# Third attention of a four-layer kernel: inverted softmax sums spread through DRAM by DMA and multiplied by GpSimd, in place of a product on TensorE

## The chip, the cores and the metric

The kernel runs as one launch on one core of a Trainium2 chip. The metric is the device time of the launch in microseconds. Before the change it is 2238.06 us, the median of three runs (2237.61 to 2240.51).

## The reference

Four layers, each an attention and a feed-forward network, are applied to 1024 rows of 256 numbers; every one of the eight parts is `x = layernorm(x + part(x))`. The change is in the third attention alone:

```python
def _L2_attn_ref(x, W_qkv, W_proj):
    ...
    SCALE = 1.0 / np.sqrt(D).astype(np.float32)
    b, s, d = x.shape
    qkv = x @ W_qkv.T
    q, k, v = jnp.split(qkv, 3, axis=-1)
    q = q.reshape(b, s, H, HD).transpose(0, 2, 1, 3)
    ...
    attn = jnp.einsum('bhqd,bhkd->bhqk', q, k) * SCALE
    causal = jnp.tril(jnp.ones((s, s), dtype=bool))
    attn = jnp.where(causal[None, None], attn, -jnp.inf)
    probs = jax.nn.softmax(attn, axis=-1)
    out = jnp.einsum('bhqk,bhkd->bhqd', probs, v)
    out = out.transpose(0, 2, 1, 3).reshape(b, s, d)
    return out @ W_proj.T
...
x = _layernorm(x + _L2_attn_ref(x, L2_attn_W_qkv, L2_attn_W_proj), axis=-1)
```

The input is one sequence of 1024 rows, so the attention is causal over all of them. There are 16 heads of 16 numbers. The softmax over the keys needs, for every head and query, the sum of the exponentials; the output of the head is divided by that sum. How the inverse of that sum reaches the 16 rows of its head is what the change alters.

## The kernel before, in words

`four_layers` runs eight stages one after the other; `attn2` is the fifth (from about 960 to 1190 us of the profile). Everything is float32, in part split into two rounded halves.

**Layout in `attn2`.** The heads are taken four at a time (`ch`, 0 to 3) and the queries in two halves of 512 (`half`). A pair (ch, half) is a unit; the units run in the order (0,0), (1,0), (2,0), (3,0), (0,1), (1,1), (2,1), (3,1). In a unit, `attend` goes over the blocks of 128 keys that the causal mask allows (4 in half 0, 8 in half 1). For a block it makes the transposed scores of two pairs of heads on TensorE into tiles of the PSUM pool `wide` (three buffers; L1629, and L1635, which adds minus the maxima), ScalarE exponentiates them into `pt` (L1641), GpSimd zeroes the masked half of a block on the diagonal (`affine_select`, L1644), and TensorE multiplies the values of the heads by `pt` into the unit's accumulator `out` (`apply`, L1616). A head has 32 rows of the accumulator: 16 of output, and row 16 of each 32 is the sum of the exponentials, because the values carry a column of ones there.

**Maxima beside it.** For a later unit, `maxima` makes the scores in the other orientation (L1582, with the mask added on TensorE by L1589) in the same three `wide` buffers, and VectorE takes their row maxima (L1593, joined by L1598). At the end of a unit's maxima, VectorE copies them (L1602), TensorE transposes them (L1605), and ScalarE and VectorE make the tile `tall` (L1608, L1609) that the unit's L1635 reads.

**What `finish` does.** When a unit's accumulator is complete, ScalarE copies it to the SBUF tile `sums` (pool `ot`, L1658). Four DMAs on SyncE's queue take the four rows of sums into `inv`, 128 partitions of 16 (L1661). After four steps VectorE inverts `inv` in one small instruction (L1667), and four DMAs put the inverses back into the rows of `sums` (L1669). Four steps later TensorE multiplies `pick` (which copies row 16 of each 32 to all 32) by `sums` into a `wide` tile (L1676; a float32 product is two passes), and VectorE multiplies `sums` by it (L1677). For ch = 3 the output projection (L1701), the residual, the layernorm and the transposes of the half follow, a step each. The last unit (3,1) has a shorter ending of its own, `finish_last`, which the change leaves alone. There are so seven calls of `finish`; below they are F1 to F7 in the order of the units.

**What sets the order.** The stage runs inside `k.in_order()`: the instructions of TensorE, VectorE, ScalarE and GpSimd stand in the order in which Python issues them. Each `yield` of the generators is one step: after every pair of heads in `attend`, the loop in `attn2` advances the maxima (`ahead`), the placing of queries and keys (`placing`), the second half's projections and values (`beside`) and the ending of the unit before (`ending`). The first `next(ending)` comes at the unit's end and the others one a step of the next unit. SyncE's DMAs are not in that written order; a scheduler places them in the one queue of SyncE, where a DMA that waits holds back those behind it. A DMA on that queue also uses one of eight semaphores in turn, so it can have to wait for the eighth DMA before it.

**Other work on the queues at the time of F1 and F2.** `second_half` stores split projections to DRAM with sixteen DMAs of 256 KB (L1531, SyncE), and GpSimd loads them back in another arrangement (`load_rows`, L1542, eight DMAs). SyncE also reloads weights of the next stage as buffers come free (L103). The tiles of `second_half` come from the pool `parts`, six buffers in a ring.

Of the kernel before, what the change touches and what calls it, by code (L numbers as in the profile page):

```python
# [28 lines left out]
ALU = mybir.AluOpType  # L29
AX = mybir.AxisListType  # L30

P = 128
# [4 lines left out]
HALF = 512  # L37
# [1367 lines left out]
def attn2(k, a):  # L1405
# [15 lines left out]
    nc = k.nc  # L1421
# [30 lines left out]
    pick = k.tile("const", [P, P], tag="pick")  # L1452
# [14 lines left out]
    projected, parts, placed, whole = {}, {}, {}, set()  # L1467
# [98 lines left out]
    def rows(j, n=32):  # L1566
        return slice(n * j, n * j + n)
# [86 lines left out]

    def finish(ch, half, out, outs):

        sums = k.tile("ot", [P, HALF])
        nc.scalar.copy(sums, out)  # L1658
        inv = k.tile("st", [P, 16], tag="inv", bufs=2)
        for j in range(4):  # L1660
            nc.sync.dma_start(  # L1661
                out=inv[rows(j), :],
                in_=sums[32 * j + 16 : 32 * j + 17, :].rearrange("p (c e) -> p c e", e=16),
            )
        for _ in range(4):
            yield
        nc.vector.reciprocal(inv, inv)  # L1667
        for j in range(4):
            nc.sync.dma_start(  # L1669
                out=sums[32 * j + 16 : 32 * j + 17, :].rearrange("p (c e) -> p c e", e=16),  # L1670
                in_=inv[rows(j), :],
            )
        for _ in range(4):
            yield
        ps = k.wide()[:, :HALF]
        nc.tensor.matmul(ps, lhsT=pick, rhs=sums, start=True, stop=True)  # L1676
        nc.vector.tensor_tensor(sums, sums, ps, ALU.mult)  # L1677
        outs.append(sums)
        yield
        if ch < 3:  # L1680
            return
        stats = k.tile("st", [P, 4, 2])
        for s in range(4):
            project_out(half, s, outs)
            yield
            k.add_stats(4 * half + s, stats)
        rstd = k.power(stats[:, :, 1], 4, LN_EPS)
        for _ in range(2):
            yield
        for s in range(4):  # L1690
            k.norm_tile(4 * half + s, stats, rstd[:, s : s + 1])
            if s % 2:
                yield
        for t in (0, 2):
            k.transpose_two(t, split=True)
            yield

    def project_out(half, s, outs):
        y = k.bank()[:, :D]
        for i in range(4):  # L1700
            nc.tensor.matmul(  # L1701
                y, lhsT=outs[i][:, s * P : (s + 1) * P], rhs=wo[:, i, :],
                start=i == 0, stop=i == 3,
            )
        k.add_rows(4 * half + s, y)
# [19 lines left out]
    with k.in_order():  # L1725
# [45 lines left out]
        for ch, half in units:  # L1771
            while (ch, half) not in found:
                next(ahead)
            out = k.bank()
            for step, _ in enumerate(attend(ch, half, out)):
                next(ahead, None)
                if half == 0 and step % 4 == 3:
                    next(ahead, None)
                if step % 2:
                    next(placing, None)  # L1780
                if (ch, half, step) > (0, 0, 1) or half:
                    next(beside, None)
                next(ending, None)
            for _ in ending:
                pass
            if (ch, half) != units[-1]:
                ending = finish(ch, half, out, outs[half])
                next(ending)
# [524 lines left out]
```

## Time and profile before

| what | value |
|---|---|
| median of three runs | 2238.06 us |
| the profiled execution, as timed | 2230.16 us |
| its span, first to last instruction | 2228.5 us |
| mean granted TensorE clock | 0.972 |
| L1676, TensorE products with `pick` | 14 passes, 7.6 us busy |
| L1677, VectorE multiplies | 7, mean 683 ns |
| L1667, VectorE reciprocals of `inv` | 7, median 242 ns |
| L1661 and L1669, gathers and scatters on SyncE's queue | 28 each, issue median 590 and 538 ns |

The profiled execution is 7.9 us below the median of the runs, and its span 1.66 us below its own time. Times in the text are microseconds from the start of the span. A row of groups reads: line, engine, operation, tile written and tiles read, shapes, count; then the busy time, the mean of one in ns, and the time for which the engine stood idle just before these instructions, with what ended it. A line of the view of waits reads: who waited, for whom, total us, times, longest. The view of windows gives the busy time of each engine in a stretch with the number of instructions, then the granted TensorE clock, the mean busy share of the DMA engines and GB/s.

Where the seven endings lie (start and end in us):

| | copy L1658 | gathers L1661 issued | inverse L1667 | scatters L1669 issued | product L1676 | multiply L1677 |
|---|---|---|---|---|---|---|
| F1 | 1020.58 | 1021.20 to 1023.71 | 1030.03 | 1030.56 to 1033.03 | 1037.09 to 1038.19 | 1038.77 |
| F2 | 1041.23 | 1041.84 to 1044.83 | 1048.25 | 1048.57 to 1051.01 | 1055.84 to 1056.96 | 1057.76 |
| F3 | 1058.54 | 1059.16 to 1061.60 | 1068.49 | 1068.76 to 1071.19 | 1074.34 to 1075.42 | 1076.14 |
| F4 | 1076.84 | 1077.45 to 1079.89 | 1082.76 | 1083.03 to 1085.47 | 1088.18 to 1089.31 | 1089.40 |
| F5 | 1110.57 | 1111.18 to 1113.62 | 1118.15 | 1118.43 to 1120.87 | 1123.87 to 1124.95 | 1125.61 |
| F6 | 1139.23 | 1139.85 to 1142.29 | 1144.97 | 1145.24 to 1147.68 | 1151.50 to 1152.52 | 1153.09 |
| F7 | 1161.44 | 1162.06 to 1164.50 | 1165.65 | 1165.97 to 1168.41 | 1169.68 to 1170.78 | 1170.82 |

### The profile page before, as it was taken

To read this page: it belongs to the slowest core of one execution; us is meant where nothing else is said; L and a number is where in the kernel's file an instruction comes from. 1 tells how busy PE (TensorE), PEld (TensorE's weight loads), DVE (VectorE), ACT (ScalarE), POOL (GpSimd) and SP (SyncE) were. 2 spreads that over 40 slices of the span, in tenths; PEclk is the share of its full clock that TensorE was granted. 3 is DMA by queue.
4 is the path that set the end of the run, shared out by engine and by line. 5 is a ranking of instruction groups with operands and counts; after the bars stand their busy time and mean duration, and the time that the engine had idled before them with its cause. 6 is when DMAs were issued, how large, how long until landed. Compare 5 with 4: busy or idle time off the path is not lost.

```text
span 2228.5 us, 24592 instructions
## 1 busy us (share of the span) xinstructions
PE 2037.2 (91%) x7893; PEld 1191.4 (53%) x7893; DVE 1299.4 (58%) x2588; ACT 849.6 (38%) x2230; POOL 522.3 (23%) x771
## 2 busy tenths in 40 slices
PE   7988768899999997988988998899999989999997
PEld 3655544576766665754434443466666665433343
DVE  6898756677777664456754444277777664222223
ACT  3656424453444433444462223654444441111111
POOL 5343131333333332402110000433333320000000
PEclk9999879999999999999999999999999999999998
DMA  6222443253545542105000000034355321222211
GB/s 183 76 72 58 136 130 109 64 148 102 145 108 161 144 103 78 38 29 181 1 2 10 29 30 0 24 95 111 93 141 125 91 53 63 76 76 84 76 65 44
DMA packets 152520, 186.88 MB, mean 84 GB/s; under 512 B 31460, under 2 KB 115240, under 8 KB 152392
## 3 DMA queue, kind: packets, MB, share of 16 engines
q1 hardware_dynamic: 142808, 160.25, 26.2%
q0 software_dynamic: 9584, 25.05, 3.7%
q8 instruction: 64, 1.05, 0.2%
q14 instruction: 64, 0.52, 0.1%
HBM read 85.24 MB, written 17.44 MB: 46 GB/s over the span
## 4 chain that ended last, share of the span: by engine, by line
PE 62%; DVE 9%; DMA 7%; ACT 3%; issue 3%; POOL 2%; SPq 1%; DVEq 0%; POOLq 0%; ACTq 0%
PE bank L159 19%; PE wide L274 9%; PE bank L408 8%; PE wide L307 6%; DMA by<-factors 5%; PE bank L166 4%; PE bank L1179 2%; DVE turned L371 2%; PE bank L1616 2%; PE bank L856 2%; PE bank L1019 1%; DMA pt<-turned 1%; PE bank L1354 1%; POOL p L267 1%; PE wide L1629 1%
## 5 line engine op out<-in xcount | busy, mean ns | idle before, releaser
L159 PE MATMUL bank<-xT,w 128*128 128x512 f32 (+2 forms) x1488 | 629.2, 563 | 4.1 <-DVE xT L185 3.0
L159 PEld LDWEIGHTS bank<-xT,w 128*128 128x128 f32 (+1 forms) x1488 | 283.1, 194 | 275.1 <-issue 254.3
L371 DVE STREAM_TRANSPOSE turned<-p 128x128 f32<-128x128 f32 (+7 forms) x232 | 283.5, 1222 | 76.0 <-DMA pt<-turned 40.3
L274 PE MATMUL wide<-k,q 128*128 128x512 f32 (+3 forms) x768 | 293.7, 492 | 18.3 <-ACT p L259 17.5
L267 POOL TENSOR_SCALAR p<-p,st 128x128 f32<-128x128 f32 (+7 forms) x256 | 190.5, 744 | 475.3 <-DVE st L266 474.8
L408 PE MATMUL bank<-pt,v 128*128 128x256 f32 x1216 | 279.4, 371 | 8.0 <-DMA pt<-turned 5.7
L408 PEld LDWEIGHTS bank<-pt,v 128*128 128x128 f32 x1216 | 225.9, 191 | 60.6 <-issue 21.0
L254 DVE TENSOR_REDUCE st<-wide 128x1 f32<-128x128 f32 (+7 forms) x256 | 193.4, 756 | 47.1 <-PE wide L279 40.1
L307 PE MATMUL wide<-t,w 128*128 128x512 f32 (+1 forms) x392 | 196.7, 626 | 17.0 <-DVE t L2205 11.8
L274 PEld LDWEIGHTS wide<-k,q 128*128 128x128 f32 x768 | 139.5, 191 | 135.3 <-issue 92.9
L259 ACT ACTIVATE p<-wide,st,factor 128x128 f32<-128x128 f32 (+7 forms) x128 | 106.4, 831 | 213.5 <-POOL st L256 210.6
L2204 DVE TENSOR_TENSOR t<-t,bank 128x512 f32<-128x512 f32 (+1 forms) x66 | 45.3, 686 | 238.8 <-PE bank L159 238.8
L259 ACT ACTIVATE p<-wide,st 128x128 f32<-128x128 f32 (+7 forms) x128 | 94.9, 741 | 230.1 <-DVE st L254 211.9
L2203 ACT ACTIVATE t<-bank 128x512 f32<-128x512 f32 (+1 forms) x66 | 39.4, 597 | 305.5 <-PE bank L159 279.5
L307 PEld LDWEIGHTS wide<-t,w 128*128 128x128 f32 (+1 forms) x392 | 67.8, 191 | 134.3 <-DVE t L2205 58.4
L779 ACT ACTIVATE e<-wide,st 128x128 f32<-128x128 f32 x256 | 90.0, 377 | 74.3 <-DVE st L787 65.6
L166 PE MATMUL bank<-w,xT 128*128 128x512 f32 (+2 forms) x288 | 118.0, 547 | 0.0
L249 DVE TENSOR_TENSOR wide<-wide,causal 128x128 f32<-128x128 f32 x192 | 55.9, 291 | 98.7 <-PE wide L274 97.5
L1641 ACT ACTIVATE pt<-wide 128x1024 f32<-128x1024 f32 (+3 forms) x96 | 75.6, 811 | 69.9 <-PE wide L1635 68.1
L166 PEld LDWEIGHTS bank<-w,xT 128*128 128x128 f32 x288 | 52.6, 196 | 44.0 <-issue 40.3
L1593 DVE TENSOR_REDUCE st<-wide 128x2 f32<-128x1024 f32 x64 | 64.3, 1020 | 20.0 <-PE wide L1589 10.2
L845 PE MATMUL bank<-w,ot 128*128 128x256 f32 x256 | 67.4, 411 | 6.8 <-ACT ot L839 5.5
(307 smaller groups left out, 2788.4 us busy)
## 6 DMA issues: line engine op xcount, KB each, us to landing
by<-factors SPq DMA_DIRECT2D x64, 256.0 KB
pt<-turned SPq DMA_DIRECT2D x60, 240.0 KB
pt<-turned SPq DMA_DIRECT2D x60, 176.0 KB
pt<-turned SPq DMA_DIRECT2D x156, 64.0 KB
w<-in_L_ffn_gate_up_dram SPq DMA_DIRECT2D x16, 512.0 KB
pt<-turned SPq DMA_DIRECT2D x28, 256.0 KB
pt<-turned SPq DMA_DIRECT2D x60, 112.0 KB
pt<-turned SPq DMA_DIRECT2D x28, 224.0 KB
```

Of the source, the lines that this page charges most:

```text
L159: self.nc.tensor.matmul(out, lhsT=weight(c), rhs=self.xcols(c, lo, n), start=c == 0, stop=c == NC - 1)
L166: self.nc.tensor.matmul(out, lhsT=self.xcols(c, lo, n), rhs=weight(c), start=c == 0, stop=c == NC - 1)
L254: nc.vector.tensor_reduce(top, scores[:, :n], axis=AX.X, op=ALU.max, negate=True)
L259: nc.scalar.activation(probs[:, :n], scores[:, :n], AF.Exp, bias=top, scale=1.0 if scale is None else scale, accum_out=total,)
L267: self.nc.gpsimd.tensor_scalar(probs[:, :n], probs[:, :n], total, 1.0, ALU.mult, ALU.mult)
L274: self.nc.tensor.matmul(s[:, lo : lo + m], lhsT=query, rhs=key(lo, m), start=True, stop=not masked or lo + m < n, skip_group_check=masked,)
L307: nc.tensor.matmul(acc[m][:, half * HALF : (half + 1) * HALF], lhsT=down[:, m * P : (m + 1) * P], rhs=h, start=i == 0, stop=i == count - 1,)
L371: k.nc.vector.transpose(squares.rearrange("p b (k q) -> p b k q", q=32), probs[:, :n].rearrange("p (k i b) -> p b k i", b=4, i=32),)
L408: self.k.nc.tensor.matmul(out.rearrange("p (a q) -> p a q", q=32) if first else out.rearrange("p (s a q) -> p s a q", s=2, q=32), lhsT=val ...
L779: nc.scalar.activation(e[:, r, f, b, :], sc[:, r, f, b, :], AF.Exp, bias=top[:, at : at + 1], accum_out=total[:, at : at + 1],)
L845: nc.tensor.matmul(y, lhsT=oT[:, i % 2 * 2 + i // 2].rearrange("p b n -> p (b n)"), rhs=wo[:, i, :], start=i == 0, stop=i == 3,)
L1641: nc.scalar.activation(two[:, :, lo:], sc[:, :, lo:], AF.Exp)
```

## The change

The four gathers stay. The inverse now comes two steps after them in place of four. One DMA stores the 128 x 16 inverses to a DRAM row for each of the four heads; two steps later one DMA reads the four rows back, each repeated to 32 partitions, into a new SBUF tile `spread` of 128 x 512 from the ring `parts`; three steps later GpSimd multiplies `sums` by it. The four scatters, the product with `pick` (and its `wide` tile) and VectorE's multiply go. From the first `next` to the multiply there are seven yields in place of eight, so that all that follows in `finish` comes a step earlier.

```diff
-        for _ in range(4):
+        for _ in range(2):
             yield
         nc.vector.reciprocal(inv, inv)
-        for j in range(4):
-            nc.sync.dma_start(
-                out=sums[32 * j + 16 : 32 * j + 17, :].rearrange("p (c e) -> p c e", e=16),
-                in_=inv[rows(j), :],
-            )
-        for _ in range(4):
+        row = k.tile("dram", [4, HALF], tag=f"inv_{ch}{half}")
+        nc.sync.dma_start(out=row.rearrange("j (p e) -> (j p) e", e=16), in_=inv)
+        for _ in range(2):
             yield
-        ps = k.wide()[:, :HALF]
-        nc.tensor.matmul(ps, lhsT=pick, rhs=sums, start=True, stop=True)
-        nc.vector.tensor_tensor(sums, sums, ps, ALU.mult)
+        spread = k.tile("parts", [P, HALF])
+        nc.sync.dma_start(out=spread, in_=row.unsqueeze(1).to_broadcast([4, 32, HALF]))
+        for _ in range(3):
+            yield
+        nc.gpsimd.tensor_tensor(sums, sums, spread, ALU.mult)
         outs.append(sums)
```

An empty line is added at the head of `finish`, so that lines below it have other numbers after the change: the copy is L1659, the gathers L1662, the inverse L1668, the store L1670, the spread L1674, the multiply L1677.

## The prediction

> **What bounds the kernel now.** I read first the busy shares, then the stage that the change touches, window by window, then the groups of its lines, the waits, and last the timeline around each of the seven endings, F1 to F7. The page:
>
> ```profile
> PE 2037.2 (91%) x7893; PEld 1191.4 (53%) x7893; DVE 1299.4 (58%) x2588; ACT 849.6 (38%) x2230; POOL 522.3 (23%) x771
> ```
>
> ```profile
> core 0: us, PE busy (x) PEld busy (x) DVE busy (x) ACT busy (x) POOL busy (x), PEclk, DMA share, GB/s
> 1020.00:1040.00 20.00, 17.71 (x123) 8.07 (x122) 13.58 (x22) 7.56 (x12) 6.25 (x12) 1.00 0.85 263
> 1040.00:1050.00 10.00, 8.83 (x72) 5.29 (x70) 6.42 (x11) 5.00 (x7) 4.51 (x8) 1.00 0.74 227
> ...
> 1110.00:1140.00 30.00, 26.08 (x205) 12.19 (x204) 22.99 (x37) 15.11 (x20) 3.24 (x8) 1.00 0.01 2
> ...
> 1160.00:1170.00 10.00, 8.43 (x65) 3.81 (x62) 0.25 (x1) 8.59 (x11) 0.77 (x2) 1.00 0.02 2
> ```
>
> TensorE is busy for 83 to 98% of each of the stage's stretches, VectorE for up to 77%; GpSimd has room. The DMA engines are nearly full from 1020 to 1050 us, where F1 and F2 lie (0.85 and 0.74), and empty after 1070. So a microsecond off TensorE is worth about one, and a wait of VectorE costs only what the three `wide` buffers don't cover. What goes:
>
> ```profile
> L1676 PE MATMUL wide<-ot,pick 128*128 128x512 f32 x14 | 7.6, 626 | 1.7 <-DMA ot<-inv 1.6
> L1677 DVE TENSOR_TENSOR ot<-ot,wide 128x512 f32<-128x512 f32 x7 | 4.8, 683 | 5.1 <-PE wide L1676 4.9
> ```
>
> The waits for the gathers, before:
>
> ```profile
> DVE inv L1667 <- DMA inv<-ot: 11.9, 1, 11.9
> ```
>
> The reciprocal waits once, in F7, where VectorE has no more maxima. In the other six the gather had landed when VectorE came to it. How narrowly is seen in F2:
>
> ```profile
> 1044.00 1.23 DVE L1593 TENSOR_REDUCE st<-wide 128x2 f32<-128x1024 f32 x1 [0.46 <-PE wide L1582]
> 1045.43 0.42 DVE L1593 TENSOR_REDUCE st<-wide 128x2 f32<-128x256 f32 x1 [0.20 <-PE wide L1589]
> 1045.89 0.16 DVE L1598 TENSOR_TENSOR tops<-st 128x2 f32<-128x2 f32 x1
> 1046.22 1.82 DVE L1593 TENSOR_REDUCE st<-wide 128x2 f32<-128x1024 f32 x2 [0.17 <-PE wide L1582]
> 1048.08 0.16 DVE L1598 TENSOR_TENSOR tops<-st 128x2 f32<-128x2 f32 x1
> 1048.25 0.25 DVE L1667 RECIPROCAL inv<-inv 128x16 f32<-128x16 f32 x1
> ```
>
> F2's last gather packet ended at 1047.64. In F7, where VectorE did wait, the packets ended at 1165.31 and the reciprocal began at 1165.65: 0.34 us from packet to start. F2's gather was thus usable at 1047.98, 0.27 us before its reciprocal.
>
> **What the skill says.** "DMA: Bandwidth & Descriptors", section "Why a DMA increments its semaphore by 16 and not by 1": a transfer is split over the largest number of engines up to 16 that divides the slowest dimension of both sides. The spread has 4 rows on its DRAM side, so 4 engines. The trace agrees in the last stage, where L2201 spreads two rows to 128 partitions, 128 packets of 2 KB at 84 ns each: on two engines that is 64 x 84 ns = 5.4 us, and its issue takes
>
> ```profile
> L2201 SPq DMA_DIRECT2D by<-factors x66: 498/4724/7113, 1838.1 to 2184.5; - x66
> ```
>
> with a median of 4.7 us[...]. On 16 engines it would be 0.7. "GPSIMD Engine Reference", section "3.1 Elementwise — side-by-side cycle accounting", has a two-input product there about twice as long as on VectorE; this trace has one of the same shape:
>
> ```profile
> L1854 POOL TENSOR_TENSOR decoded<-sign,scales x24: 1261/1272/1285, 434.8 to 866.5; 128x512 f32<-128x512 f32 x24
> ```
>
> "SBUF — State Buffer", section "SBUF: two separate sides", says that GpSimd and a two-input VectorE operation exclude each other; VectorE's two-input operations here (L1598) are 0.16 us long, so I cost it at 0 (up to 0.2 in all).
>
> **Part 1, TensorE's product goes.** Two passes take 1.0 to 1.1 us. F4, F5, F6: the next work follows at once; 1.06 + 1.00 + 0.95 = 3.0. F1: after it the chain of maxima waits for VectorE (L1605 waited 0.99 for L1602), so what is saved is L1677's 0.68 ahead of L1602; 0.65. F2, F3: VectorE runs without a gap just after, so between 0.65 and 1.06; 0.8 each. F7: TensorE also waited 1.25 for the scatter and ScalarE then 2.53 for TensorE, so both go: 2.3. Sum 3.0 + 0.65 + 1.6 + 2.3 = 7.6 (if each gave its all, 7.7 + 1.7 = 9.4). VectorE's 4.8 us are worth only the part counted here.
>
> **Part 2, the reciprocal moves two steps up.** Now the gather is what VectorE waits for; behind it in VectorE's order stand the maxima, and behind them TensorE's next `wide` tile. The order of the built instructions gives the new place; from the timeline, when VectorE would be there, and when the gather is usable (last packet + 0.34):
>
> F1 1024.33 against 1024.86; F2 1045.23 against 1047.98; F3 1062.41 against 1062.75; F4 1080.38 against 1081.04; F5 1115.64 against 1114.78; F6 1142.78 against 1143.44; F7 unchanged.
>
> Waits of 0.5, 2.75, 0.3, 0.7, 0, 0.7. What reaches TensorE: F1 0.4, since L1602 stands right behind and L1605 waits for it. F3, F4, F6: the next maximum used to wait 0.2 to 0.5 for TensorE anyway and the reciprocal's own 0.24 leaves its old place; with three buffers TensorE notices 0.2, 0.2 and 0.3. F2 is the large one: the tile after next must go into the buffer that the delayed maximum (old start 1045.43) still holds, so TensorE, at 1046.0, stops until 1048.7: 2.7. It can be more: the gather's fourth DMA now waits by its semaphore for the 512 KB reload (before, for a 256 KB store), and F1's spread sits ahead of it on four engines; 0 to 2 more, I take 0.6, so 3.3. Less is possible if the queues drain sooner (2.0). Sum 0.4 + 3.3 + 0.2 + 0.2 + 0.3 = 4.4; bounds 2.6 and 7.
>
> **Part 3, store, spread and GpSimd.** Quiet queues: the store lands 1.65 us after issue (the same kind, L1984: issue 1836.36, SyncE free of its wait at 1837.98); the spread's first packet comes 1.37 after issue (L2201: 1838.09 to 1839.46), 32 packets on each of four engines take 2.7, and 0.35 to the semaphore: 4.4. Inverse to spread is 6.1 us, with the product 7.4. On SyncE the spread waits for the store, holding back whatever follows: in F1 two stores of `second_half` (whose data come later anyway), in F2 a reload; 0. GpSimd's queue behind the multiply has the `affine_select`s, and TensorE's L1616 waits for them. F2, F3: GpSimd comes to the multiply at 1055.1 (+2.7) and 1073.8, the spreads land near 1056.6 (full queues, 4 us more) and 1069; 0. F4: product done at 1088.7; the projection, now at the place of L1676 (1088.2), needs this head group as its fourth, 1.3 us later; 0, and 0.5 if late. F5 to F7 have over 4 us or no selects near. F1 is tight: spread issued near 1029 behind about 1 MB, 4 us of queue, 2.7 of packets, half again for GpSimd's loads beside it: near 1037. The multiply then ends at 1038.4, the select at 1038.8, and L1616 wants it by 1040.1. Cover 1.2 us; 0. The 28 small scatters that go lighten the queues; 0.
>
> **Sum.** -7.6 + 4.4 + 0 = -3.2 us against the profiled execution's 2230.16 us (span 2228.5), so 2227.0 there; the median of the runs is 7.9 above that execution, and the difference carries over: 2238.06 - 3.2 = 2234.9.
>
> **Rivals.** A: the early reciprocal costs nearly nothing, as the gathers land earlier with 28 DMAs gone and VectorE 4.8 us lighter. For it: four of the waits are under 0.7 us. Against: F2's gather was late behind GpSimd's loads, which stay. Then -7.6 + 1 = -6.6: 2231.5. B, slower: F1's spread drowns in the full queues. Place: GpSimd, its multiply ahead of the last select of unit (1,0). It costs from a landing at 1038.3 on, one for one at L1616; and F2's first gather waits by its semaphore for this same spread, so beyond 1041.5 F2's reciprocal moves too. Landing at 1045 costs 6.7 and puts F2's gather about 3 later: -3.2 + 9.7 = +6.5, 2244.6. For it: DMA share 0.85 and L2201's slow kind. Against: F1's scatters, issued at 1030.56, were done at 1036.49. That the change doesn't do what it says is excluded by the order of the instructions.
>
> **How the numbers follow.** My forecast 0.52 (own range 2231.5 to 2238.5), A 0.23, B 0.25 (from 2238.5 to 2246). The range takes A from 2230 and B to 2242.5. A measurement of this kernel tells about 0.2%, 4.5 us, from no change, so faster is below 2233.6: A's 0.22 and 0.10 of the forecast, 0.32; slower is above 2242.5: half of B, 0.14; the rest 0.54.
>
> **What would show it.** The reciprocal's row idle for the gather in F1, F2, F4, F6, longest in F2 (3 us), with TensorE idle there; no gap of TensorE in F7 near 1168; spreads of 4.4 us in F3 to F7; no L1616 waiting for GpSimd in F1. Wrong would make me: F2's wait under 1 us, or above 6; L1616 idle on L1644; TensorE's wait at L1701 in F4.

## The result and the profile after

The changed kernel takes 2241.89 us (median of 20 runs, 2237.17 to 2250.01) against 2237.91 for the kernel before in the same set (20 runs, 2233.33 to 2242.46): ratio 1.002, 95% interval 1.001 to 1.0029. It is about 4 us slower, clear of the noise, where 3.2 us less was predicted. The profiled execution of the changed kernel took 2238.66 us (span 2236.7) against 2230.16, so these two stand 8.5 us apart; part of that is chance, as will be seen. In what follows, differences in us are of medians; the ratios and their 95% intervals are taken from all the runs and can stand up to 2 us away from them.

From F1's copy to the copy of the last unit the stage took 159.13 us before and 163.97 after. The page after, engine totals:

```profile
PE 2036.8 (91%) x7879; PEld 1192.9 (53%) x7879; DVE 1294.2 (58%) x2581; ACT 850.2 (38%) x2230; POOL 530.7 (24%) x778
```

TensorE has 14 instructions fewer, but 0.4 us less to do and not 7.6. The view of windows, the changed kernel, stretches that answer to those of before (moved by 4.8 us at F1 and about 9 at the end):

```profile
core 0: us, PE busy (x) PEld busy (x) DVE busy (x) ACT busy (x) POOL busy (x), PEclk, DMA share, GB/s
1025.34:1045.34 20.00, 16.60 (x112) 7.91 (x112) 12.94 (x20) 7.56 (x12) 7.46 (x13) 0.96 0.81 251
1045.34:1055.34 10.00, 9.31 (x47) 5.71 (x46) 5.95 (x10) 4.95 (x6) 3.58 (x7) 0.50 0.74 235
1119.00:1149.00 30.00, 26.66 (x213) 12.44 (x211) 22.15 (x35) 17.20 (x22) 4.52 (x9) 1.00 0.04 11
1169.00:1179.00 10.00, 9.74 (x76) 4.35 (x80) 0.25 (x1) 8.74 (x10) 0.25 (x1) 1.00 0.07 17
```

The second row is what the prediction did not have. TensorE is busy 93% of it and does only 47 products in 10 us, where the row of before for 1040 to 1050 has 72: its granted clock (the column after POOL) is 0.50, half of full speed, for the whole stretch. "Half clock" below means this. The groups of the changed kernel between 985 and 1195 us (last column: idle time ahead, and for whom):

```profile
L1677 POOL TENSOR_TENSOR ot<-ot,parts 128x512 f32<-128x512 f32 x7 | 8.9, 1272 | 54.4 <-DMA parts<-inv 51.6 <-DMA rows<-parts 2.8
...
L1598 DVE TENSOR_TENSOR tops<-st 128x2 f32<-128x2 f32 x32 | 6.5, 203 | 1.1
L1605 PE MATMUL wide<-ident,tops 128*128 128x128 f32 x32 | 5.8, 310 | 8.7 <-DVE tops L1602 8.7
...
L1602 DVE COPY tops<-tops 128x8 f32<-128x8 f32 x16 | 2.8, 205 | 0.0
L1668 DVE RECIPROCAL inv<-inv 128x16 f32<-128x16 f32 x7 | 1.8, 251 | 17.3 <-DMA inv<-ot 17.3
```

The same groups before:

```profile
L1598 DVE TENSOR_TENSOR tops<-st 128x2 f32<-128x2 f32 x32 | 5.5, 173 | 1.1
...
L1605 PE MATMUL wide<-ident,tops 128*128 128x128 f32 x32 | 5.0, 280 | 5.4 <-DVE tops L1602 4.2 <-ACT pt L1641 1.2
...
L1602 DVE COPY tops<-tops 128x8 f32<-128x8 f32 x16 | 2.5, 185 | 0.0
```

GpSimd's multiply and the late inverse are there as expected. New are three things: TensorE waits 8.7 us, not 4.2, for VectorE's copies L1602 ahead of its transposes L1605; the small operations L1598 and L1602 have become slower on average; and in F7 L1616 waits 2.00 us for GpSimd.

**A pause and what follows it.** The changed kernel's TensorE ahead of L1605 of unit (3,0), then two windows, the first over that pause (3.41 us), the second after it:

```profile
1041.24 0.28 PE L1589 MATMUL wide<-causal_b,ident_b 128*128 128x128 bf16 x2
1041.45 0.64 PE L1616 MATMUL bank<-pt,v 128*32 128x256 f32 x8
1044.55 1.09 PE L1605 MATMUL wide<-ident,tops 128*128 128x128 f32 x4 [2.46 <-DVE tops L1602]
```

```profile
1040.39:1043.80 3.41, 1.52 (x16) 0.51 (x14) 3.41 (x5) 0.17 (x1) 0.76 (x1) 1.00 0.99 299
1043.80:1057.46 13.66, 12.21 (x54) 7.86 (x54) 7.04 (x13) 4.95 (x6) 5.39 (x10) 0.50 0.76 234
```

The same place before, with full clock after it:

```profile
1039.75 0.63 PE L1605 MATMUL wide<-ident,tops 128*128 128x128 f32 x4 [0.99 <-DVE tops L1602]
```

In this stage of the traces the half-clock stretches are 3.4 us long or multiples of that, 6.8, 10.2, 13.7 and once 17.1, and in each trace they all begin on one grid of 3.41 us, which lies differently against the program from trace to trace. The Trainium skill, "TensorE: Matmul & The Clock Gate", section 'Part 1: The HAM clock gate (the "warmup" mystery)', describes this: TensorE's clock is halved after an idle window of about 3.4 us, and the windows run free of the program. The traces agree on the length and on the free running. They differ in that a window needn't be idle (TensorE was busy for 1.52 of 3.41 us above), and there the measurement decides. I divided all 17 traces of this study into those windows (30 to 2200 us of each) and counted in each the columns of its products, a product weighted by the share of the 128x128 array that it uses (32 columns of weights count a quarter, 64 rows a half; a well-filled window has some 4,000):

```
weighted columns in a window at full clock   windows   followed by half clock
under 900                                        119   119
900 to 1200                                      148   135
1200 to 1500                                     237    33
1500 to 2100                                     324    16
over 2100                                       9282    23
```

All 23 windows of the last row lie between 952 and 1090 us, so in this stage the weighting does not tell the windows apart well. The time for which TensorE was busy in the window does so at least as well: half clock followed all 198 full-clock windows with under 1.25 us of it, 107 of the 290 with 1.25 to 2 us and 21 of the 9622 with more; in the stage alone (985 to 1200 us) 10 of 10, 24 of 31 and 7 of 945. The traces so show that too little work in a window brings half clock. They don't show that a narrow product counts less than a full one.

So a pause of 2.5 us, with 1.5 us of work around it, is enough if a window happens to lie over it. As the windows run free, the same kernel meets it in some executions and not in others: in F7 of the changed kernel half clock followed a pause of 2.0 us in one trace, and none followed a pause of 1.8 us in the other. A good part of the scatter of the times goes with this: among the 65 runs of the kernel before in the third set below, each thousandth of the whole launch's mean clock goes with 1.1 us (the slope; the correlation is -0.76).

### The profile page after: what moved, and what is told of

It reads as the page before. It is cut to its first block, busy times and chain, and to the rows that moved or that the text cites. A ratio compares the mean times of both kernels' runs of the same rounds, so it can differ in the third digit from the quotient of the medians.

```text
span 2236.7 us, 24533 instructions
## 1 busy us (share of the span) xinstructions
PE 2036.8 (91%) x7879; PEld 1192.9 (53%) x7879; DVE 1294.2 (58%) x2581; ACT 850.2 (38%) x2230; POOL 530.7 (24%) x778
## 4 chain that ended last, share of the span: by engine, by line
PE 60%; DVE 10%; DMA 8%; ACT 3%; issue 3%; POOL 2%; SPq 1%; DVEq 0%; POOLq 0%; ACTq 0%
PE bank L159 18%; PE wide L274 9%; PE bank L408 8%; PE wide L307 6%; DMA by<-factors 5%; PE bank L166 4%; PE bank L1179 2%; DVE turned L371 2%; PE bank L856 2%; DMA pt<-turned 2%; PE bank L1616 1%; PE bank L1019 1%; PE bank L1354 1%; POOL p L267 1%; PE wide L1582 1%
```

## The experiments

Three theories. Clock: the time that TensorE saves is spent waiting at L1605 for VectorE, which has not become faster, and the longer pauses halve its clock. Wait: the new waits alone cost it. Queue: the spread is late or GpSimd's multiply is in the way. Each kernel was compared with the kernel before on the same chip in the same set; the kernel before itself had medians from 2237.45 to 2244.59 in these sets, so each difference is taken within a set, and two kernels of different sets are compared by these differences. "Stage" is from F1's copy to the last copy in the profiled execution; "lost" is the time in it times the share of clock not granted (3.4 us of half clock is 1.7 lost). An "idle product" is one whose result nobody reads.

**First set: undo or do one part.** The control:

> The kernel before, unchanged, against itself: the size of the scatter, and the granted clock of each of its runs, which the page of one execution doesn't give. All theories: 0 us within about 2. The clock theory (half-clock stretches of TensorE are what the changed kernel loses by) expects a mean clock near 0.970 here, clearly above the 0.9635 of the changed kernel's runs; the wait theory (the early reciprocal and GpSimd's late product make TensorE wait) has no need of it and expects about the same 0.964.

Measured: 2245.16 against 2242.96, ratio 1.0003 (0.9994 to 1.0013). Mean clock 0.966 and 0.967, lower than the 0.970 that the clock theory expected but above the changed kernel's 0.9636. Stage 160.61 us, 5.1 lost; before's first profile 159.13, 3.4 lost. Six of its seven units agree with that profile to 0.02 us; the third, F3 to F4, is 1.46 longer, with 1.7 more lost. So a unit's length is a fine measure as long as the clock is named beside it.

The changed kernel with the inverse at four steps:

```diff
-        for _ in range(2):
+        for _ in range(4):
             yield
         nc.vector.reciprocal(inv, inv)
```

> The changed kernel with the reciprocal and all that follows it back at four steps after the copy (nine yields to the product in place of seven). Wait theory: the early reciprocal holds up VectorE, so some 4 us come back: 3 to 5 us below the changed kernel, near or a little below the kernel before. Clock theory: the reciprocal's place matters little, 0 to 1.5 us, and the kernel stays 3 to 4 us above the one before with a mean clock near 0.9635. Queue theory (the spread's late landing holds GpSimd's selects): the spread lands two steps later but the product is also two steps later, so 0.

Measured: +8.0 us (1.0034, 1.0021 to 1.0046; five runs), mean clock 0.960. All theories missed. The inverse no longer waits (but in F7), and yet nothing comes back. The clock is 0.0072 lower than that of the kernel before; at 1.1 us per thousandth that is an estimate of 7.9 us, the whole difference. Three pauses at L1605 are 1.82, 1.82 and 2.35 us, stage 159.75 with 8.5 lost.

The kernel before with only the inverse (and scatters) two steps up:

```diff
-        for _ in range(4):
+        for _ in range(2):
             yield
         nc.vector.reciprocal(inv, inv)
...
-        for _ in range(4):
+        for _ in range(6):
             yield
         ps = k.wide()[:, :HALF]
```

> The kernel before with only the reciprocal and the scatters moved two steps up; the product with pick and VectorE's multiply stay in their places. Wait theory: 4 us slower than the kernel before (F2 most, TensorE idle there about 3 us). Clock theory: 0 to 1 us. Queue theory: 0.

Measured: +8.5 us (1.0036, 1.0024 to 1.0049), mean clock 0.9637 against 0.967. That is more than any of the three theories had. The waits of VectorE for the gather are the predicted ones, F2's (timeline of VectorE):

```profile
1064.97 0.25 DVE L1667 RECIPROCAL inv<-inv 128x16 f32<-128x16 f32 x1 [1.98 <-DMA inv<-ot]
```

But the stage, 162.38, is only 1.8 above the control's 160.61 at the same 5.1 lost, nearly all in F2 (19.19 us to F3's copy against 17.31). The lower clock is worth an estimated 3.6 us. The other 3 us are not shown by this execution; the pauses at L1605 grew to 1.50 and 2.33 us.

The kernel before without the product:

```diff
-        ps = k.wide()[:, :HALF]
-        nc.tensor.matmul(ps, lhsT=pick, rhs=sums, start=True, stop=True)
-        nc.vector.tensor_tensor(sums, sums, ps, ALU.mult)
         outs.append(sums)
```

> The kernel before without the product with pick and without VectorE's multiply in the seven endings: it leaves out the division by the sums for those seven units; gathers, reciprocal and scatters stay. It is the upper bound of what the change can take off TensorE. By the prediction's part 1: 7.6 us below the kernel before (6.5 to 9.4). Clock theory: less, 2 to 5 us, with a lower mean clock than the kernel before[...].

Measured: -3.2 us (0.9994, 0.9986 to 1.0003), mean clock 0.9637. By the ratio it is less still, and the interval reaches no gain at all: less than half of the 7.6, with the lower clock, as the clock theory has it. Why the clock was lower this set doesn't show; the windows above point to the longer pause at (3,0), 1.82 us for 0.99. From F4 on, where its trace has no half clock, the four units are shorter by 0.94, 0.90, 0.84 and 2.35 us; the prediction had 1.06, 1.00, 0.95 and 2.3.

**Second set: the pause filled, and the pause made longer.** Products that nobody reads, in the wait:

```diff
         ps = k.wide()[:, :HALF]
+        if (ch, half) in ((3, 0), (0, 1), (3, 1)):
+            for _ in range(4):
+                nc.tensor.matmul(
+                    ps, lhsT=keys[0][:, 0, :P], rhs=queries[0][:, 0, :HALF],
+                    start=True, stop=True, skip_group_check=True,
+                )
         for s in range(4):
             nc.tensor.transpose(ps[:, s * P : (s + 1) * P], top[:, s, :], k.ident)
```

> The changed kernel with four idle products (keys by queries, 128x128 by 512 columns, into the wide tile that the transposes then overwrite) put on TensorE ahead of the transposes L1605 of the units (3,0), (0,1) and (3,1), where its trace has TensorE waiting 2.46, 2.52 and 2.09 us for VectorE; they lie in the wait. Clock theory (such a pause leaves a window of about 3.4 us nearly without work, after which TensorE is granted half its clock for 3.4 to 13.7 us): the half-clock stretches behind these three places go, the mean clock comes up to 0.967 or more, 5 to 8 us faster than the changed kernel, so 1 to 4 us below the kernel before. Wait theory (the pauses themselves are the whole cost): 0 to 1 us slower than the changed kernel, clock as it was.

Measured: level with the kernel before (2238.66 against 2238.58; 1.0004, 0.9992 to 1.0015), mean clock 0.9676 against 0.9679. TensorE does more work than in the changed kernel, and that kernel's 4 us above the kernel before are gone. The 1 to 4 us below it that the clock theory had were not reached. Its TensorE at the same place as above, and the windows over the pause and after it:

```profile
1042.02 0.64 PE L1622 MATMUL bank<-pt,v 128*32 128x256 f32 x8
1042.58 1.19 PE L1606 MATMUL wide<-q,k 128*128 128x512 f32 x4
1044.83 0.66 PE L1611 MATMUL wide<-ident,tops 128*128 128x128 f32 x4 [1.05 <-DVE tops L1602]
```

```profile
1040.40:1043.80 3.40, 3.19 (x24) 1.49 (x24) 3.40 (x4) 0.72 (x2) 0.80 (x2) 1.00 1.18 302
1043.80:1057.50 13.70, 9.72 (x74) 5.74 (x74) 7.80 (x15) 5.65 (x8) 5.91 (x11) 1.00 0.94 285
```

VectorE's copies come hardly earlier (L1605 at 18.93 us after F1's copy against 19.22 in the changed kernel, and 18.75 in that kernel's second trace, of the third set below, where the clock was halved too), but the clock stays whole, and after it 74 products are done in the time of 54.

> The same four idle products at the same three places in the kernel before, whose pauses are 0.99, 1.89 and 1.16 us. Clock theory: less to gain, the 3.4 us of lost clock behind (0,1) at most: 1 to 4 us below the kernel before. Wait theory: 0 to 1 us slower.

Measured: +0.4 us (1.0, 0.9988 to 1.0011), clock 0.9684 against 0.9679. The clock theory's 1 to 4 us did not come. In the stage the filling is longer than the pause at (3,0) and costs 0.6 us, and at (0,1) it gives 1.9 (157.75 with nothing lost, against 159.13 with 3.4); of this nothing is seen in the median. It is also the fair partner of the filled changed kernel: filled against filled, 2238.66 against 2238.97, the change is worth 0.3 us, within the noise.

> The changed kernel with the late inverse (four steps), which measured 8 us above the kernel before at a mean clock of 0.960, with the idle products ahead of L1605 of (3,0), (0,1), (1,1) and (3,1) (pauses of 1.82, 1.82, 2.35 and 1.17 us). Clock theory: clock back to 0.967 or more and 8 us or more faster than without them: 0 to 5 us below the kernel before. Wait theory: no faster than 2250.

Measured: -2.5 us (0.9991, 0.9982 to 1.0001), clock 0.9670. Without the filling the same kernel was 8.0 above the kernel before: 10 us back by 4.8 us of idle products (four take 1.19 us, at four places). Stage 155.50, 1.7 lost; with the early inverse (the first filled kernel) it is 157.63 at the same 1.7, so 2.1 more, of which F2 has 1.7 (18.00 against 16.26). These two kernels also differ in the filling at (1,1) and in the place of all that follows the inverse, so the 2.1 are not the inverse's alone.

The other direction, the kernel before with VectorE held up:

```diff
         both = top.rearrange("p s (h i) -> p s h i", h=2)
+        if (ch, half) in ((3, 0), (0, 1)):
+            high = k.tile("parts", [P, HALF], F32R, tag="high", bufs=1)
+            full = queries[0][:, 0, :HALF].bitcast(F32)
+            for _ in range(2):
+                nc.vector.tensor_tensor(high, full, full, ALU.mult)
```

> The other way round: the kernel before with two idle multiplies of 128x512 (about 0.7 us each) on VectorE ahead of the copies L1602 of the units (3,0) and (0,1), so that TensorE's pauses there grow from 0.99 and 1.89 to about 2.4 and 3.3 us. Wait theory: the added 2.8 us and no more, clock as in the kernel before. Clock theory: 2.8 us and about 5 to 10 us more from half-clock stretches behind both places, with a mean clock near 0.963.

Measured: +5.25 us (1.0024, 1.0011 to 1.0037), mean clock 0.9646 against 0.9679. The pauses became 2.42 and 3.16 us. Windows over the second and after it:

```profile
1077.20:1080.60 3.40, 0.89 (x8) 0.40 (x6) 3.33 (x5) 0.81 (x1) 0.81 (x2) 1.00 0.00 0
1080.60:1094.30 13.70, 12.73 (x64) 5.58 (x64) 7.56 (x15) 2.65 (x5) 1.62 (x4) 0.50 0.01 1
```

The pauses explain 2.7 us (1.43 and 1.27 more); the clock, 0.0033 lower, is worth an estimated 3.6. The time lies between the wait theory's 2.8 and the clock theory's 7.8 to 12.8, and its interval (2.5 to 8.3 us) reaches both; what decides for the clock theory is the clock itself, which the wait theory had unchanged.

**Third set: how large the terms are with a whole clock.**

```diff
         sums = k.tile("ot", [P, HALF])
...
-        nc.gpsimd.tensor_tensor(sums, sums, spread, ALU.mult)
         outs.append(sums)
```

> The filled kernel with the late inverse (2236.1 us, 2.5 below the kernel before), without GpSimd's multiply; it leaves out the division by the sums for the seven units. Store and spread stay. It prices the multiply's hold on GpSimd's selects and on the projection. Part 3 of the prediction put that at 0. If it is 0: within 1 us of the filled kernel. If GpSimd's wait for the spread (0.87 us in F7, 7.23 in F1, 2.7 and 3.3 in F2 and F3) reaches TensorE: 1 to 3 us faster.

Measured: -8.8 us (0.9955, 0.9939 to 0.9971), clock 0.9694 against 0.9685; 6.3 us beyond the one with the multiply (of the second set), more than the 1 to 3 expected. In the stage 150.11 with nothing lost against 155.50 with 1.7: 3.7 us of GpSimd's multiply itself, of them 1.7 in F7, 1.1 in F4, 0.7 in F6, three units that have the whole clock in both.

> The kernel before without the product and VectorE's multiply (it leaves out the division for the seven units; 3.2 us below the kernel before at a mean clock of 0.9637 against 0.967), with four idle products ahead of L1605 of (3,0), (0,1) and (3,1). Clock theory: the clock comes back to 0.967 or more and the gain of part 1 shows nearly whole: 6 to 9 us below the kernel before. Wait theory (part 1 was simply too large): no faster than the 3.2 us without the fill.

Measured: -7.2 us (0.9964, 0.9952 to 0.9977), clock 0.9681 against 0.9685. The kernel before without the product, once more, but with the pauses filled: the 3.2 us have become 7.2, and the stage has no half clock. That agrees with Part 1's 7.6; against the kernel before with the same filling, whose stage has no half clock either, the stage is 9.0 shorter (148.70 against 157.75), of which 0.6 is what the filling costs at (3,0) there.

> The changed kernel, unchanged, on the same chip as the others of this set: about 4 us above the kernel before (2 to 6), with a mean clock 0.003 to 0.004 below that of the kernel before's own runs (clock theory) or the same (wait theory).

Measured: +5.65 us (1.0021, 1.0008 to 1.0034), clock 0.9637 against 0.9685 in the same set. The clock of the changed kernel is lower by 0.0048, in 22 runs against 65.

A version built on this, the changed kernel with

```diff
-        for _ in range(2):
+        for _ in range(3):
             yield
         nc.vector.reciprocal(inv, inv)
...
-        nc.gpsimd.tensor_tensor(sums, sums, spread, ALU.mult)
+        eng = nc.vector if (ch, half) == (2, 1) else nc.gpsimd
+        eng.tensor_tensor(sums, sums, spread, ALU.mult)
```

and idle products ahead of L1605, four, two and three:

> A version meant to beat both: the changed kernel with the inverse at three steps (eight yields to the multiply, so that the second half's ending stands where it stood before), idle products ahead of L1605 of (3,0), (0,1) and (3,1) (four, two and three), and F7's multiply on VectorE. Clock theory: 3 to 7 us below the kernel before with a mean clock of at least 0.967. Wait theory: level with the kernel before or slower.

Measured: -5.6 us (0.9971, 0.9957 to 0.9985), clock 0.9681. It beats the kernel before, and the changed kernel, 5.65 above that in the same set. Its profiled execution still met a half clock of 17.1 us at (0,1), where only two products fill.

**Fourth set: by what the multiply costs.** In the changed kernel, F6, VectorE's timeline and GpSimd's:

```profile
1156.07 1.23 DVE L1593 TENSOR_REDUCE st<-wide 128x2 f32<-128x1024 f32 x1 [0.79 <-PE wide L1589]
1157.33 1.09 DVE L1598 TENSOR_TENSOR tops<-st 128x2 f32<-128x2 f32 x1
1158.34 0.29 DVE L1602 COPY tops<-tops 128x8 f32<-128x8 f32 x2
```

```profile
1157.13 1.26 POOL L1677 TENSOR_TENSOR ot<-ot,parts 128x512 f32<-128x512 f32 x1 [12.32 <-DMA parts<-inv]
```

In the same place of the kernel before:

```profile
1150.51 0.16 DVE L1598 TENSOR_TENSOR tops<-st 128x2 f32<-128x2 f32 x1
1150.59 0.29 DVE L1602 COPY tops<-tops 128x8 f32<-128x8 f32 x2
```

In the changed kernel L1598 ends when GpSimd's multiply ends (1158.42 and 1158.39), and TensorE's pause at the L1605 behind it is 2.09 us in place of 1.16. In F1 the copy L1602 took 0.80 us, in F6 of the second trace of the changed kernel 1.25, and in F6 of its filled version:

```profile
1154.75 1.24 DVE L1602 COPY tops<-tops 128x8 f32<-128x8 f32 x1
```

In the traces without a multiply on GpSimd no L1598 or L1602 of this stage takes over 0.44 us. And F7's end, TensorE and GpSimd:

```profile
1180.42 0.34 PE L1635 MATMUL wide<-tall,ones 64*128 64x384 f32 x2
1182.76 1.05 PE L1616 MATMUL bank<-pt,v 128*32 128x512 f32 x6 [2.00 <-POOL pt L1644]
```

```profile
1181.07 1.27 POOL L1677 TENSOR_TENSOR ot<-ot,parts 128x512 f32<-128x512 f32 x1 [11.82 <-DMA parts<-inv]
1182.29 1.49 POOL L1644 TENSOR_SCALAR_AFFINE_SELECT pt<-pt 128x256 f32<-128x256 f32 x4
```

The select waits behind the multiply, the multiply for the spread, and TensorE for the select. The next two put the multiply on VectorE, with the filling and without:

```diff
-        nc.gpsimd.tensor_tensor(sums, sums, spread, ALU.mult)
+        nc.vector.tensor_tensor(sums, sums, spread, ALU.mult)
```

> The changed kernel with the idle products ahead of L1605 (level with the kernel before) and the seven multiplies on VectorE in place of GpSimd. Shared-side theory (VectorE's L1598 and L1602 stand still while GpSimd multiplies): these stay at 0.16 us, L1605 comes 0.5 to 0.9 us earlier in F1 and F6, 2 to 4 us faster than the same on GpSimd. Late-spread theory (the spread's landing is what costs, whichever engine waits for it): VectorE now waits for it with the maxima behind, 0 to 3 us slower than on GpSimd.

Measured: 1.0007 (0.9996 to 1.0018), clock 0.9642 against 0.9669: no gain in the sum, as the late-spread theory had it. From F4's copy to the end it is 99.52 us against 103.65 with the multiply on GpSimd (1.7 lost there), so 2.4 to 4.1 better, and L1598 and L1602 are short again:

```profile
1165.99 0.16 DVE L1598 TENSOR_TENSOR tops<-st 128x2 f32<-128x2 f32 x1
1166.07 0.69 DVE L1683 TENSOR_TENSOR ot<-ot,parts 128x512 f32<-128x512 f32 x1
1166.68 0.24 DVE L1602 COPY tops<-tops 128x8 f32<-128x8 f32 x2
```

But in F1 VectorE now stands 1.94 us for the spread with the maxima behind it, TensorE's pause is 3.24 us despite the filling, and the clock halves for 13.7 us. Each of the two theories holds, at a different ending.

> The changed kernel with the seven multiplies on VectorE and no idle products. Shared-side theory: the pauses ahead of L1605 shrink by 0.5 to 0.9 us in F1 and F6, so less half clock too: 3 to 6 us faster than the changed kernel, near the kernel before. Late-spread theory: as slow as the changed kernel or slower.

Measured: +6.1 us (1.0027, 1.0017 to 1.0037), clock 0.9604: slower than the changed kernel, as the late-spread theory allowed. Without the filling F1's pause is 4.57 us. VectorE at F1:

```profile
1058.81 0.69 DVE L1677 TENSOR_TENSOR ot<-ot,parts 128x512 f32<-128x512 f32 x1 [2.06 <-DMA parts<-inv]
```

Last, eight yields, the inverse after (2 in F1, 4 in F2, 3 elsewhere), the multiply on VectorE but for F2's, and four idle products ahead of L1605 of (0,0), (3,0), (0,1) and (3,1):

```diff
+        steps = {(0, 0): (2, 3, 3), (1, 0): (4, 2, 2)}.get((ch, half), (3, 2, 3))
...
+        eng = nc.gpsimd if (ch, half) == (1, 0) else nc.vector
+        eng.tensor_tensor(sums, sums, spread, ALU.mult)
```

> A second version meant to beat both: eight yields; the inverse at two steps in F1, four in F2 and three in the others; multiplies on VectorE but for F2's; four idle products ahead of L1605 of (0,0), (3,0), (0,1) and (3,1). By the stage's rows without clock loss some 149 to 152 us from F1's copy to the last, 5 to 9 us below the kernel before, clock 0.968 or more; the first candidate was 6.5 below.

Measured: 2233.84 us against 2244.59 (0.9956, 0.9941 to 0.9972; seven runs), clock 0.9687 against 0.9669. Its stage, with the whole clock (column after POOL):

```profile
1031.33:1182.44 151.11, 137.28 (x1036) 67.64 (x1036) 97.22 (x160) 79.50 (x105) 30.75 (x66) 1.00 0.24 71
```

Both versions beat the kernel before, each in its own set, and so the changed kernel, which was slower than it in two sets. Their intervals overlap, so which of the two is better is not settled.

## Why the prediction was wrong, point by point

- **Part 1, -7.6 us: near.** 7.2 us with the pauses filled, and the units F4 to F7 to within 0.12 us each. With both kernels filled the stage gives 9.0; 0.6 of that is the filling's own cost in F1, and F2 and F3 were taken too small (1.1 and 1.7, for 0.8 each).
- **What the parts left over as longer pauses: here the prediction failed.** The step is that a longer pause of TensorE was priced at no more than its own length. For F1 it says that after the product "the chain of maxima waits for VectorE (L1605 waited 0.99 for L1602)", and counts only 0.65 of the 1.1 us; the rest is TensorE waiting longer, and what follows from that was put at nothing. The wait of L1605 for L1602 went from 4.2 us to 8.7, and by all three parts. At (3,0) (F1) TensorE comes earlier by the product, while the copies end at 19.07 us after F1's copy, as late as before (19.02), because GpSimd holds them; the kernel without product has 18.43. At (0,1) (F3) they end at 7.27 and not 6.62, by the early inverse (the inverse early alone: 7.06). At (3,1) (F6) at 12.60 and not 11.65, held by GpSimd. So pauses of 0.99, 1.89 and 1.16 became 2.46, 2.52 and 2.09, and such a pause can halve the clock for 3.4 to 13.7 us. The mean clock is 0.9637 against 0.9685; 0.0048 at 1.1 us per thousandth is an estimate of 5.3 us. The prediction read the clock only as a column that said 1.00 at 1020 and 1040, though the trace of before has 6.8 us of half clock from 1066.5 on, behind its longest pause (the window over that pause and the stretch after it):

```profile
1063.10:1066.50 3.40, 1.51 (x14) 0.87 (x16) 2.03 (x5) 1.25 (x2) 0.41 (x1) 1.00 0.00 0
1066.50:1073.30 6.80, 6.48 (x38) 2.61 (x30) 3.94 (x6) 1.70 (x4) 0.81 (x2) 0.50 0.02 1
```

- **Part 2, +4.4: the mechanism right, the size too large.** Predicted waits of VectorE 0.5, 2.75, 0.3, 0.7, 0, 0.7; measured with the early inverse alone 0.58, 1.98, 0.25, 0.67, 0.01, 0.67. What reached TensorE, clock apart, is 1.8 (up to 2.1 from the filled pair), for 4.4: F2's share was 1.9 for 3.3, and the small waits of F1, F3, F4 and F6 cost it nothing measurable. In the changed kernel's own trace F2's wait is 0; there the clock is halved from before F2's copy on and all of TensorE's work comes later, while in the filled kernel, with the whole clock, the wait is 1.84. F4's wait is 1.8 to 1.9 us in the changed kernel and its filled version, for 0.67 with the early inverse alone; why is not shown.
- **Part 3, 0: wrong by 3.7 us.** The prediction named the shared side of SBUF (the Trainium skill, "SBUF — State Buffer", section "SBUF: two separate sides") and costed it "at 0 (up to 0.2 in all)", because VectorE's operations there are 0.16 us long. What counts is how long GpSimd's operation still runs: L1598 and L1602 took 0.8 to 1.25. The section puts VectorE operations in a two-port mode, such as a float32 copy within SBUF, beside the two-input ones, and the copy L1602 was held like L1598. It also said for F7 "no selects near": the last unit's steps are so short that its first select is, and 2.00 us are waited. F4's projection waited 0.4 us for GpSimd, for 0 and 0.5 if late. The transfers themselves came nearly as predicted: in F5 to F7 the multiply began 4.9 to 5.3 us after the spread's issue, for 4.4. And the multiply's own price was read rightly, 1.27 us for 0.69 on VectorE; the figure behind "about twice as long" is one for an addition.
- **Sum.** Clock apart the parts add up to -7.2 + 1.8 + 3.7 = -1.7. The direct measure is filled against filled: -0.3 us in the median, and in the stage -0.1 with 1.7 more lost (157.63 against 157.75). So even with the whole clock the -3.2 would have been 1.5 to 3 us too low, and that it would have come so near is luck: Part 2 was 2.6 too large and Part 3 3.7 too small. With the clock's estimated 5.3 us the parts come to +3.6, against +4.0 and +5.65 measured.
- **The rivals.** B put its loss at F1's spread. The spread was issued at 1035.57 and multiplied at 1043.04. F1's copy lies 4.76 us later in this trace, so on the prediction's times that is 1030.8 and 1038.3, hardly later than its 1029 and 1037, and no L1616 waited there; TensorE waited for VectorE at the same time. B's sign was right, its mechanism not. A was nearer on Part 2 (1.8 us, for its 1 and the forecast's 4.4) and fails on Part 3 and the clock.

Open: of the lower mean clock the single executions show 3.4 to 8.5 us lost more inside the stage, while 0.0048 of the launch is 10.8; the filling, which touches only the stage, brings nearly all of it back (0.9676 against 0.9679). Outside the stage single executions lose between 59 and 82 us, so one trace can't account for 10.8. Why the unfilled late inverse and the early inverse alone fall to 0.960 and 0.9637 with such pauses is not shown window by window: one execution of each was traced, and its windows lie where they happen to. The filling shows that the low clock hangs on these pauses. Whether TensorE's busy time or the size of its products decides in a window stays open.

## What to carry to other kernels

Where TensorE is the bound and another engine's chain meets it now and then, time taken off TensorE comes back as a longer pause at the meeting point; look at each pause that grows, and ask whether some 3.4 us around it can be left with less than some 2 us of work, because then the next 3.4 to 13.7 us may run at half clock, as they did here. A few idle products in the pause tell whether that is so, and may be worth keeping. Moving an elementwise operation to an idle GpSimd was not free for VectorE: its small operations L1598 and L1602, when they met the multiply, lasted until GpSimd was done with it. Compare such versions over many runs and by their mean clock, since one trace shows only where its own windows lay.

## What the runs showed of the hardware

- Half clock follows too little work, not too much: after all 198 windows of 3.41 us in which TensorE was busy for under 1.25 us, and after 21 of 9622 in which it was busy for 2 us or more (17 traces, windows at full clock).
- Sixteen products that nobody reads, 0.3 us each, made a kernel some 10 us faster (the late inverse, +8.0 to -2.5, each against the kernel before in its own set, on two chips).
- A copy of 128x8 on VectorE took 1.25 us beside a GpSimd multiply of 1.27, and 0.16 to 0.17 in most other places.
